# Layer 0's products in the edge stage of a four-layer graph network: first group of the fifth batch, or its third

## The chip, the cores and the metric

The kernel runs on one core of one Trainium2 chip, as one launch. The metric is the device time of the whole program in microseconds (us). TensorE is called PE here, VectorE DVE, ScalarE ACT, GpSimd POOL, SyncE SP, as the profile calls them.

## The reference, cut to what matters

Four graph layers over N = 3125 nodes with 128 features and E = 103125 directed edges (50000 drawn, both ways, and one loop for each node). Each layer is followed by a residual and a layer norm. Layer 0 is the one that matters here:

```python
xw = x @ weight
msgs = edge_val[:, None] * xw[edge_col]
out = jax.ops.segment_sum(msgs, edge_row, num_segments=N_NODES)
out = jax.nn.relu(out + b)
...
x = _layernorm(x + out)
```

Layer 1 is an attention layer over the same edges, layer 2 an attention layer that uses dot products, layer 3 two mean aggregations with products of weights.

## The kernel before

**Dense matrices in place of edges.** The kernel pads the nodes to 25 blocks of 128. It first turns the edge list into two 3200 x 3200 matrices in DRAM: `wd`, the edge weights in float32, one row for each target node, and `ctd`, the edge counts in bfloat16. After that every layer is a set of dense matrix products over these. For layer 0 the product is (block i of `wd`) transposed times (block i of `xw`), added up in PSUM over i = 0 to 24.

**The edge stage (lines 837 to 958).** The edges are sorted, and cut into 640 windows of five nodes (`WN = 5`). A batch is 16 windows, and the loop `for b in range(NBT)` (L897) has 40 batches; the last holds 4 windows. In each batch:

- `make(b + 1)` (called at the head of the loop) lets DVE build the one-hot matrices of the next batch: `ohd` and `ohc` (L865), then three `wod` (L876), which hold the weights in three bfloat16 parts. `ohd` and `ohc` have two buffers and `wod` has six, so DVE can be one batch ahead: the `ohd` of batch b + 2 needs that PE has read the `ohd` of batch b for the last time.
- The batch is worked through in four groups, k = 0, 4, 8 and 12, of four windows each. I write (b, k) for a group. PE makes the counts `cp` (8 matmuls, L911) and the weights `wp` (24 matmuls, L919). ACT copies them out as `cs` (L924) and `ws` (L930), and between the two it makes part of the next batch's `wod` (`cur[3](k)`, L882, four instructions). `cp` and `wp` share three PSUM buffers.
- After a batch, SP stores `ws` to `wd` (L941, two DMAs, 896 and 104 KB) and after each second batch `cs` to `ctd` (L944, 1000 KB).

**Layer 0's products inside the edge stage.** A row block of `wd` is complete as soon as the batches that hold its 128 rows are stored (80 rows a batch). So the stage already multiplies such blocks, on PE between the groups. `adds0` (L809 to 823) loads one row block into two tiles of ten column blocks (`cw`, L816, two DMAs of 640 KB, from a pool with four buffers) and returns 20 closures. Each is one product: a float32 matmul into PSUM at L820, which the trace shows as two passes. They go into the list `todo`. After each group the loop takes up to three from the head of the list and runs them. It then requests the next row block if the list holds 20 or fewer and the rows are stored:

```python
if order:
    m = min(3, len(todo)) if b > 3 else 0
    for f in todo[:m]:
        f()
    del todo[:m]

    if len(todo) <= 20 and (done + 1) * P <= (b - 1) * BW * WN:
        todo += adds0(zp, done, acc0, (0, Z0))
        done += 1
```

I call the two loads for one value of `done` "load 0" to "load 24". What the loop leaves over is run after it, and the remaining blocks follow (`for f in todo`, then `add0` for `range(done, NB)`). Then come layer 0's ends (`end0`), the products of the other five column blocks (`left`, also L820), and layer 1.

**What sets the order.** From the end of batch 2 on, PE and SP work in program order, written by hand (`manual_schedule`). The order on ACT and DVE is a planner's, which plans with its own cost model.

Of the kernel before, what the change touches and what calls it, by code (L numbers as in the profile page):

```python
# [510 lines left out]
def fast_path(  # L511
# [238 lines left out]
    def products_of_weights():  # L750
        nc.gpsimd.tensor_tensor(both, gb_row, sb_row, OP.add)
        tw = {}
        for name, w in (("l1", l1_wt), ("q", wqt), ("k", wkt), ("v", wvt)):
            t = zps.tile([P, P], F32, name="trw", tag="acc3")
            nc.tensor.transpose(t, w, ident)
            tw[name] = ep.tile([P, P], F32, name="tw_" + name)
            nc.scalar.copy(tw[name], t)
        t = zps.tile([P, P], F32, name="trw", tag="acc3")
        nc.tensor.matmul(t[:, 0 : 2 * H], tw["l1"], att, start=True, stop=True)
        nc.scalar.copy(watt, t[:, 0 : 2 * H])  # L760
        t = zps.tile([P, P], F32, name="trw", tag="acc3")
        nc.tensor.matmul(t, tw["q"], tw["k"], start=True, stop=True)
        nc.scalar.copy(wyv[:, 0:P], t)
        t = zps.tile([P, P], F32, name="trw", tag="acc3")
        nc.tensor.matmul(t, tw["v"], wot, start=True, stop=True)
        nc.scalar.copy(wyv[:, P:], t)

    def xw_of(b0, n):

        t = zps.tile([P, 512], F32, name="trx", tag="acc0")  # L770
        for k in range(n):
            nc.tensor.transpose(t[:, k * P : (k + 1) * P], x[:, b0 + k, :], ident)
        xT = ep.tile([P, 512], F32, name="f_xTb")
        nc.scalar.copy(xT[:, : n * P], t[:, : n * P])
        t = zps.tile([P, 512], F32, name="trx", tag="acc2")
        for k in range(n):
            nc.tensor.matmul(t[:, k * P : (k + 1) * P], xT[:, k * P : (k + 1) * P], l0_wt, start=True, stop=True)
        nc.scalar.copy(xw[:, b0 : b0 + n, :].rearrange("p b d -> p (b d)"), t[:, : n * P])
# [30 lines left out]
    def adds0(pool, i, accs, blocks):  # L809

        b0, n = blocks
        steps = []
        for h in range(0, n, 10):
            m = min(10, n - h)
            cw = pool.tile([P, min(10, n), P], F32, name="cw")[:, 0:m]
            nc.sync.dma_start(  # L816
                cw.rearrange("p c d -> p (c d)"), wd[i * P : (i + 1) * P, (b0 + h) * P : (b0 + h + m) * P]
            )
            for j in range(h, h + m):
                steps.append(lambda j=j, a=cw[:, j - h, :]: nc.tensor.matmul(  # L820
                    accs[j // 4][:, j % 4, :], a, xw[:, i, :], start=False,
                    stop=(i == NB - 1 and (j % 4 == 3 or j == n - 1)), skip_group_check=True,
                ))
        return steps
# [16 lines left out]
    def make(b):  # L841

        if b % 8 == 1 and 8 < b < NBT - 8:
            keys[b // 8 + 1] = columns_of(b // 8 + 1)
        if b % 8 == 3 and 8 < b < NBT - 8:
            keys[b // 8 + 1] = keys_of(*keys[b // 8 + 1])
        kd2, kc2, w2, w3 = keys[b // 8]
        ohd = op_.tile([P, 2 * BW, P], BF16, name="ohd")
        ohc = op_.tile([P, 2 * BW, P], BF16, name="ohc")

        def twos(k):
            k = k[:, b % 8, :, :, :].rearrange("p q w t -> p (q w) t")
            return k[:, :, None, :].to_broadcast([P, 2 * BW, P // 2, 2])

        def some(s):
            if b < NBT - 1:
                return [slice(0, 2 * BW if s < 2 else BW)]
            return [slice(0, LW)] + ([slice(BW, BW + LW)] if s < 2 else [])

        def packed(o, ww):  # L860
            return o[:, ww].rearrange("p w (a t) -> p w a t", t=2)

        for o, k in ((ohd, kd2), (ohc, kc2)):
            for ww in some(0):
                nc.vector.tensor_tensor(  # L865
                    packed(o, ww), twos(k)[:, ww],
                    ramp.rearrange("p (a t) -> p a t", t=2)[:, None, :, :].to_broadcast(
                        [P, ww.stop - ww.start, P // 2, 2]
                    ),
                    OP.is_equal,  # L870
                )
        wod = []
        for s in range(3):
            f = of_.tile([P, 2 * BW, P], BF16, name="wod")
            for ww in some(s):
                tip[s] = nc.vector.tensor_tensor(packed(f, ww), packed(ohd, ww), twos(w2[s])[:, ww], OP.mult)  # L876
            wod.append(f)

        def more(k):
            for w in range(k, k + 4):  # L880
                at = (b % 8) * BW + w
                nc.scalar.activation(wod[2][:, BW + w, :], ohd[:, BW + w, :], AF.Copy, scale=w3[:, 1, at : at + 1])  # L882

        return ohd, ohc, wod, more
# [4 lines left out]
    todo = []  # L889
# [6 lines left out]
    for b in range(NBT):  # L896
        ohd, ohc, wod, _ = cur  # L897
        cur = make(b + 1) if b + 1 < NBT else None
        nw = BW if b < NBT - 1 else LW
        if b % SB == 0:  # L900
            cs = sp.tile([P, NB, SB * BW * WN], BF16, name="cs")
            if b + SB == NBT:
                nc.gpsimd.memset(cs[:, :, ((SB - 1) * BW + LW) * WN :], 0.0)
        ws = sp.tile([P, BW, P], F32, name="ws")
        for k in range(0, nw, 4):
            cp = cps.tile([P, 4, P], F32, name="cp", tag="cw")
            wp = cps.tile([P, 4, P], F32, name="wp", tag="cw")
            for j in range(4):
                for q in range(2):
                    w = q * BW + k + j  # L910
                    nc.tensor.matmul(  # L911
                        cp[:, j, 0:KW], ohd[:, w, :], ohc[:, w, 0:KW], start=(j == 0 and q == 0), stop=(j == 3 and q == 1),
                        skip_group_check=True,
                    )
            for j in range(4):
                for q in range(2):
                    w = q * BW + k + j
                    for s in range(3):
                        made = nc.tensor.matmul(  # L919
                            wp[:, j, :], ohc[:, w, :], wod[s][:, w, :], start=(j == 0 and q == 0 and s == 0),  # L920
                            stop=(j == 3 and q == 1 and s == 2), skip_group_check=True,
                        )
            i0 = (b % SB) * BW * WN + k * WN
            nc.scalar.copy(  # L924
                cs[:, :, i0 : i0 + 4 * WN].rearrange("p c (w i) -> p c w i", i=WN),
                cp[:, :, 0:KW].rearrange("p w (i c) -> p c w i", c=NB),
            )
            if cur and (b + 1 < NBT - 1 or k < LW):
                cur[3](k)
            nc.scalar.copy(ws[:, k : k + 4, :], wp)  # L930
            if order:
                m = min(3, len(todo)) if b > 3 else 0
                for f in todo[:m]:
                    f()
                del todo[:m]
# [4 lines that stand above are left out]
        for a, e in ((0, 112), (112, KW)):  # L940
            nc.sync.dma_start(wv_[b * BW : b * BW + nw, a:e, :].rearrange("w k d -> k w d"), ws[a:e, 0:nw, :])  # L941
        if b % SB == SB - 1:
            i0 = (b - SB + 1) * BW * WN
            nc.sync.dma_start(ctd[:, :, i0 : i0 + SB * BW * WN].rearrange("c d i -> d c i"), cs)  # L944
        if b < 2:
            for blocks in GB[4 * b : 4 * b + 4]:
                xw_of(*blocks)
        if b == 2:
            with tc.issue_after(made.ins):
                products_of_weights()  # L950
            acc0 = [zps.tile([P, 4, P], F32, name=f"acc{k}", tag=f"acc{k}") for k in range(Z0 // 4)]
            for a in acc0:
                bias0(a, 4)

            order = ExitStack()
            order.enter_context(tc.manual_schedule(engines={mybir.EngineType.PE, mybir.EngineType.SP}))
# [446 lines left out]
    with ExitStack() as st:  # L1403
# [82 lines left out]
        for x_, (q, c) in enumerate(items):  # L1486
# [17 lines left out]
            elif c == NB - 1:  # L1504
                for k0 in range(0, n, 3):
                    m = min(3, n - k0)
# [3 lines left out]
                for k0 in range(0, n, 3):  # L1510
                    m = min(3, n - k0)
# [4 lines left out]
                    for j in range(m):  # L1516
                        b = i0 + k0 + j
# [258 lines left out]
```

## Time and profile before

| What | us |
|---|---|
| three runs, median (lowest to highest) | 1503.28 (1501.07 to 1508.55) |
| the profiled execution, its own time | 1507.44 |
| its span, first to last instruction | 1505.6 |
| PE busy / DVE busy / ACT busy in that span | 1395.4 / 978.8 / 914.3 |
| the first product of layer 0 on PE starts at | 88.07 |
| the edge stage's last group ends, with its products, at about | 463.9 |
| the last product into `acc0` ends at | 490.74 |

The profile gives each instruction's start and duration in us from the span's start. A row of the timeline merges equal neighbours (x24 is 24 instructions), and ends with the idle time of the engine before it and what ended that idle time, in brackets. The chain of waits is followed back from the last instruction: at each step it shows what the program was waiting for. The view by stretch gives, for each stretch of time, the busy time of the engines, the granted share of PE's clock (PEclk, 1.00 is full), the busy share of the DMA engines and the GB/s that they moved.

### The profile page before, as it was taken

Reading aid. Unit: us, or ns where it says so; the run is one execution under the profiler, and the core shown is the slowest. Engines: PE = TensorE matmul, PEld = TensorE weight load, DVE = VectorE, ACT = ScalarE, POOL = GpSimd, SP = SyncE. Lnnn points to the kernel's source line nnn. Section 1 sums busy time; section 2 is a strip of 40 time slices with the busy share of each in tenths; the row PEclk is TensorE's granted clock in tenths of the full one; section 3 lists DMA queues with packets and bytes.
Section 4 is the critical chain, followed back from the end, with each engine's and each line's share of the span. In section 5 each row is a group of like instructions: output and inputs, shape, how many; then the busy total and the mean of one; then the engine's idle time right before and its main releaser. Section 6 shows DMA issues by size and latency. Waiting matters only on the chain.

```text
span 1505.6 us, 34986 instructions
## 1 busy us (share of the span) xinstructions
PE 1395.4 (93%) x14775; PEld 1227.3 (82%) x14775; DVE 978.8 (65%) x1575; ACT 914.3 (61%) x1865; POOL 128.9 (9%) x164
## 2 busy tenths in 40 slices
PE   3889999999998988998979989899999999999996
PEld 3889999999998878987978989677777774458996
DVE  4989899999991389898888879534464352012005
ACT  2978789888882489878867787454555331023005
POOL 1000000000000012132032113200000000000000
PEclk8999999999999999999999999999999999999998
DMA  7368789989887733443433534332222218512551
GB/s 206 96 179 226 198 221 242 234 213 230 238 218 221 222 115 114 125 124 113 135 90 112 142 88 117 115 121 70 69 60 81 71 47 309 200 53 114 197 174 46
DMA packets 209700, 223.91 MB, mean 149 GB/s; under 512 B 72956, under 2 KB 183339, under 8 KB 209277
## 3 DMA queue, kind: packets, MB, share of 16 engines
q1 hardware_dynamic: 208748, 218.51, 50.6%
q8 instruction: 117, 1.92, 0.5%
q0 software_dynamic: 400, 1.97, 0.4%
q10 hardware_dynamic: 385, 1.11, 0.2%
q14 instruction: 50, 0.41, 0.1%
HBM read 157.19 MB, written 64.36 MB: 147 GB/s over the span
## 4 chain that ended last, share of the span: by engine, by line
PE 72%; DVE 11%; ACT 8%; DMA 4%; issue 2%; POOL 2%; SPq 0%; ACTq 0%; DVEq 0%; POOLq 0%
PE wp L919 10%; PE acc L1302 9%; PE acc L1453 9%; PE s L1445 8%; PE acc L1553 7%; PE acc L1629 6%; PE acc L820 6%; PE acc L1297 5%; PE cp L911 3%; DVE cm L1287 3%; ACT wod L882 3%; PE left L820 2%; DMA cw<-wd 2%; ACT fm L1286 1%; DVE cm L1280 1%
## 5 line engine op out<-in xcount | busy, mean ns | idle before, releaser
L1302 PE MATMUL acc<-vp,cm 128*128 128x198 bf16 x2500 | 344.5, 252 | 8.2 <-DVE cm L1287 6.7
L1297 PE MATMUL acc<-vp,ct 128*128 128x204 bf16 x1250 | 317.1, 255 | 10.1 <-DVE vp L1205 4.5
L1286 ACT ACTIVATE fm<-adr,bas 128x768 bf16<-128x768 f32 (+1 forms) x320 | 287.2, 953 | 61.9 <-DVE cm L1287 60.1
L1302 PEld LDWEIGHTS <-cm 128*128 128x128 bf16 x2500 | 236.4, 98 | 25.2 <-DVE cm L1287 8.8
L919 PE MATMUL wp<-wod,ohc 128*128 128x128 bf16 x3768 | 239.6, 220 | 7.1 <-ACT cs L924 5.4
L919 PEld LDWEIGHTS <-ohc 128*128 128x128 bf16 x3768 | 220.9, 99 | 8.7 <-issue 8.3
L876 DVE TENSOR_TENSOR wod<-ohd,w 128x4096 bf16<-128x4096 bf16 (+2 forms) x122 | 221.4, 1867 | 0.4 <-PE wp L919 0.4
L1287 DVE TENSOR_TENSOR cm<-fm,ct 128x768 bf16<-128x768 bf16 (+1 forms) x320 | 202.6, 664 | 28.8 <-PE acc L1302 13.9
L882 ACT ACTIVATE wod<-ohd,wu 128x128 bf16<-128x128 bf16 x628 | 197.7, 397 | 0.0
L1449 DVE TENSOR_TENSOR e<-e,ct 128x416 f32<-128x416 f32 (+1 forms) x175 | 108.0, 623 | 110.4 <-ACT e L1448 102.8
L1448 ACT ACTIVATE e<-s,f_nm 128x416 f32<-128x416 f32 (+1 forms) x175 | 109.6, 633 | 103.1 <-PE s L1445 95.7
L1453 PEld LDWEIGHTS acc<-self__8043,e 128*128 128x128 f32 x1250 | 148.2, 192 | 19.8 <-issue 18.9
L820 PE MATMUL acc<-f_xw,cw 128*128 128x128 f32 x1000 | 147.8, 289 | 11.9 <-DMA cw<-wd 11.9
L1453 PE MATMUL acc<-self__8043,e 128*128 128x129 f32 x1250 | 148.5, 276 | 0.0
L1445 PE MATMUL s<-yT,f_xT 128*128 128x416 f32 (+1 forms) x350 | 143.1, 544 | 4.5 <-ACT rt L1425 2.6
L820 PEld LDWEIGHTS acc<-f_xw,cw 128*128 128x128 f32 x1000 | 127.7, 198 | 12.5 <-DMA cw<-wd 12.5
L1297 PEld LDWEIGHTS <-ct 128*128 128x128 bf16 x1250 | 122.1, 98 | 4.0 <-issue 2.7
L924 ACT CAST cs<-cp 128x500 bf16<-128x500 f32 x157 | 90.7, 578 | 39.5 <-PE cp L911 39.5
L1445 PEld LDWEIGHTS s<-yT,f_xT 128*128 128x128 f32 x350 | 62.5, 191 | 55.4 <-issue 40.7
L865 DVE TENSOR_TENSOR ohd<-kd,ramp 128x4096 bf16<-128x4096 bf16 (+1 forms) x41 | 90.1, 2200 | 20.3 <-PE cp L911 18.6
L930 ACT COPY ws<-wp 128x512 f32<-128x512 f32 x157 | 90.2, 579 | 20.9 <-PE wp L919 20.6
L911 PE MATMUL cp<-ohc,ohd 128*128 128x125 bf16 x1256 | 96.3, 220 | 3.7 <-ACT ws L930 3.5
(341 smaller groups left out, 1520.6 us busy)
## 6 DMA issues: line engine op xcount, KB each, us to landing
ct<-f_ctd SPq DMA_DIRECT2D x46, 800.0 KB
wd<-ws SPq DMA_DIRECT2D x39, 896.0 KB
cw<-wd SPq DMA_DIRECT2D x50, 640.0 KB
ct<-f_ctd SPq DMA_DIRECT2D x150, 192.0 KB
f_ctd<-cs SPq DMA_DIRECT2D x20, 1000.0 KB
ct<-f_ctd SPq DMA_DIRECT2D x50, 224.0 KB
ct<-f_ctd SPq DMA_DIRECT2D x25, 416.0 KB
ct<-f_ctd SPq DMA_DIRECT2D x25, 365.2 KB
```

The costliest lines, as they stand in the source:

```text
L820: steps.append(lambda j=j, a=cw[:, j - h, :]: nc.tensor.matmul(accs[j // 4][:, j % 4, :], a, xw[:, i, :], start=False, stop=(i == NB - 1 a ...
L876: tip[s] = nc.vector.tensor_tensor(packed(f, ww), packed(ohd, ww), twos(w2[s])[:, ww], OP.mult)
L882: nc.scalar.activation(wod[2][:, BW + w, :], ohd[:, BW + w, :], AF.Copy, scale=w3[:, 1, at : at + 1])
L911: nc.tensor.matmul(cp[:, j, 0:KW], ohd[:, w, :], ohc[:, w, 0:KW], start=(j == 0 and q == 0), stop=(j == 3 and q == 1), skip_group_check=True,)
L919: made = nc.tensor.matmul(wp[:, j, :], ohc[:, w, :], wod[s][:, w, :], start=(j == 0 and q == 0 and s == 0), stop=(j == 3 and q == 1 and s ...
L1286: nc.scalar.activation(f[:, : n * P], at, AF.Relu, bias=bas[:, c, h : h + 1], scale=UP)
L1287: nc.vector.tensor_tensor(m[:, : n * P], f[:, : n * P], ct[:, : n * P], OP.min)
L1297: nc.tensor.matmul(out_(F1, PW), ct[:, k * P : (k + 1) * P], vp[:, c, hp : hp + 2, :, 2 * F1 : V1], start=(c == 0), stop=False, skip_group ...
L1302: nc.tensor.matmul(out_(0, 2 * F1)[:, j], ms[j][:, k * P : (k + 1) * P], vp[:, c, hp + j, :, 0 : 2 * F1], start=False, stop=(c == NB - 1 a ...
L1445: nc.tensor.matmul(s[:, :m], xT[:, c * P : (c + 1) * P], yT[:, i0 * P + a : i0 * P + a + m], start=True, stop=True)
L1448: nc.scalar.activation(e[:, a : a + m], s[:, :m], AF.Exp, bias=nm[:, q : q + 1], scale=scale)
L1453: nc.tensor.matmul(acc[k // 3][:, (k % 3) * (P + 1) : (k % 3 + 1) * (P + 1)], es[q, c][:, k * P : (k + 1) * P], vo[:, c, 0 : P + 1], start ...
```

## The change

The products begin at group (4, 8) in place of (4, 0). The pair (b, k) is compared as Python compares tuples, so groups (4, 8), (4, 12) and all groups of later batches are in, and (4, 0) and (4, 4) are not.

```diff
             if order:
-                m = min(3, len(todo)) if b > 3 else 0
+                m = min(3, len(todo)) if (b, k) > (4, 4) else 0
                 for f in todo[:m]:
                     f()
                 del todo[:m]
```

Nothing is added to or taken from the computation: the same 500 products run in the same order, six of them later.

## The prediction

> **What bounds the kernel now.** I read the chain of waits first: PE holds 72% of it, and in the edge stage two of its longest pieces are not work but transfers of `cw`:
>
> ```profile
> 100.02 7.29 DMA cw<-wd
> ...
> 136.90 10.70 DMA cw<-wd
> ```
>
> Then PE's timeline around these two:
>
> ```profile
> 101.31 0.60 PE L911 MATMUL cp<-ohc,ohd 128*128 128x125 bf16 x8
> ...
> 103.09 0.66 PE L820 MATMUL acc<-f_xw,cw 128*128 128x128 f32 x4
> 107.35 0.80 PE L820 MATMUL acc<-f_xw,cw 128*128 128x128 f32 x2 [3.59 <-DMA cw<-wd]
> ...
> 112.64 0.60 PE L911 MATMUL cp<-ohc,ohd 128*128 128x125 bf16 x8
> ...
> 142.68 0.60 PE L911 MATMUL cp<-ohc,ohd 128*128 128x125 bf16 x8
> ...
> 147.64 1.65 PE L820 MATMUL acc<-f_xw,cw 128*128 128x128 f32 x6 [3.02 <-DMA cw<-wd]
> ...
> 153.70 0.60 PE L911 MATMUL cp<-ohc,ohd 128*128 128x125 bf16 x8
> ```
>
> The reader is to see that the third product of group (5, 8) waits for load 1, and the first of (9, 0) for load 3. Between them PE has no wait over 0.15 us. Then the view by stretch, for the clock after a wait and for the steady state:
>
> ```profile
> 107.40:112.60 5.20, 5.20 (x40) 5.14 (x41) 3.31 (x2) 1.16 (x2) 0.00 (x0) 0.51 0.01 5
> ...
> 166.00:169.00 3.00, 1.98 (x29) 1.80 (x27) 2.76 (x6) 3.00 (x10) 0.00 (x0) 1.00 0.93 183
> ...
> 180.00:200.00 20.00, 20.00 (x307) 19.91 (x305) 20.00 (x11) 17.34 (x49) 0.00 (x0) 1.00 0.89 228
> ```
>
> The seventh number is the granted clock: about half for the 5 us behind the first wait, and full across an idle time of 1.02 us (166 to 169). The last row is the steady state: PE and DVE are both busy for all 20 us. A group starts each 2.505 us on PE, so a batch takes 10.02; DVE makes a batch in 10.0 (2.20 + 2.20 + 5.6). So what PE gains counts only as far as DVE follows, and I need DVE's idle times, from its timeline:
>
> ```profile
> 109.09 2.29 DVE L865 TENSOR_TENSOR ohd<-kd,ramp 128x4096 bf16<-128x4096 bf16 x1 [3.89 <-PE cp L911]
> ...
> 111.58 2.29 DVE L865 TENSOR_TENSOR ohc<-kc,ramp 128x4096 bf16<-128x4096 bf16 x1 [0.20 <-PE wp L919]
> ...
> 120.86 2.29 DVE L865 TENSOR_TENSOR ohd<-kd,ramp 128x4096 bf16<-128x4096 bf16 x1 [1.45 <-ACT wod L882]
> ...
> 156.91 2.29 DVE L865 TENSOR_TENSOR ohd<-kd,ramp 128x4096 bf16<-128x4096 bf16 x1 [5.99 <-PE cp L911]
> ```
>
> These are all of DVE's waits between 85.3 and 168; from there to 250 it waits 0.24 in all.
>
> **The change, part by part.** *What moves.* No instruction or DMA is added or removed. Six products (12 passes) leave groups (4, 0) and (4, 4), and the list is six longer from then on. I followed `todo` by hand through both versions. Load 1 is requested at (5, 0) in both, but needed at (6, 0) instead of (5, 8); load 3 is requested at (8, 0) in both, and needed at (9, 8) instead of (9, 0). So each gets two groups more, 5.0 us. From load 2 on, each load has 6 or 7 groups between request and need (before: 4 to 7). Many later requests come one to three groups later, because the list must first fall to 20. At the end 417 products are taken instead of 423, and the list holds 23 after (39, 0): load 22, requested at (38, 12) before, now comes after the loop, in SP's queue behind the stores of batches 38 and 39 and the last `ctd` store.
>
> *What the waits cost PE.* From the `cp` of (5, 8) to that of (6, 0) 112.64 - 101.31 = 11.33 us pass where 2 x 2.505 = 5.01 are normal: 6.32, of which 3.59 is the wait and the rest the half clock. From (9, 0) to (9, 8) it is 153.70 - 142.68 - 5.01 = 6.01. Sum 12.3, and the six products give another 2 x 0.72 = 1.45 at the front, where 0.72 is the chain's piece for six passes.
>
> [...]
>
> *Whether the waits go.* DVE starts batch 5 at 85.22, before the first product at 88.07, so this start stays. With no waits it goes on without a break: batch 6 is made at 105.2, as now. PE then runs `wp` of (6, 0) to 106.6, and its third product comes at about 107.0. Load 1 landed at 100.02 + 7.29 = 107.31. Its issue follows batch 4's store, which waits for ACT's last `ws` of batch 4; this can be 0 to 1.45 earlier. So load 1 lands at 105.9 to 107.3, and a wait of 0 to 0.3 is left: short enough to keep the clock, by the 1.02 above. Load 3: batch 9 is made at 105.2 + 30.1 = 135.3, so the first product of (9, 8) comes at 135.3 + 5.0 + 1.3 = 141.6. Its issue came 2.2 after the last `ws` of batch 7 started; that `ws` now starts at about 124.2, so the issue is at 126.4, and with the same 10.7 it lands at 137.1, with 4.5 to spare.
>
> *What DVE leaves of it.* DVE can win back its idle times, 3.89 + 0.20 + 1.45 + 5.99 = 11.5, and no more, since it runs on without a break to 250. PE could give 13.8, so DVE is the bound: batch 11's `ohd` starts at 145.4 instead of 156.9, and the stage runs 11.5 earlier from there. Later waits (PE for ACT's `cs` or `ws`, 0.5 to 1.0 each) stay. The end of the loop comes 11.5 earlier; if later stretches in which PE leads let it use its 2.3 of advance, up to 12.
>
> *The tail of layer 0.* The rows of PE's timeline:
>
> ```profile
> 463.22 4.68 PE L820 MATMUL acc<-f_xw,cw 128*128 128x128 f32 x40
> 467.74 1.28 PE L807 MATMUL left<-l_br,ones 128*128 128x128 f32 x10
> 468.85 4.63 PE L820 MATMUL acc<-f_xw,cw 128*128 128x128 f32 x40
> 478.79 11.95 PE L820 MATMUL acc<-f_xw,cw 128*128 128x128 f32 x80 [5.30 <-DMA cw<-wd]
> ```
>
> Today 40 products run, then PE waits 5.30 for load 23, and 40 more follow in 11.95 (the first at half clock). After the change, and in the clock of before, 26 run, PE is ready at 470.2, waits for load 22, and then has 60: 11.95 + 20 x 0.226 (4.52 us for 40 passes at full clock in the chain) = 16.5. When does load 22 land? At the latest when load 23 did, at 478.8: the end is then 495.3, which is 4.5 later than 490.74. But load 23 had load 22's 1.28 MB ahead of it in the queue, and load 22 does not: at the 413 GB/s of the stretch 478 to 481 that is 3.1, so it lands at about 475.5 and the end is 492.0, 1.3 later. At best the stores also start a little earlier (the issue of load 22 held SP from 456.59 to 462.0) and the cost is 0. The value is 1.0, ends 0 and 4.5. Load 24 needs load 22's buffers, free about 4.5 to 8 us after PE resumes, and is needed 12 us after: with 4 us from issue to landing in an empty queue it is in time.
>
> [...]
>
> *Sum.* -11.5 + 1.0 = -10.5, from 1507.44 to 1496.9 for a profiled execution. The median of the runs is 4.16 below the profiled time; the same step gives 1503.28 - 10.5 = 1492.8. Behind layer 0 everything shifts; where half-clock windows fall may change, so I allow 2 us either way.
>
> **The rivals.** *Part stays.* Load 1 still lands over 1 us late and the clock halves again (the spare is only 0), or the tail pays 4.5. The first costs at most 6.3, less the 2.3 that PE has in hand, so 4; either way the gain is about 7, together 3: 1496 to 1500. For it speaks the thin spare of load 1; against it, that its issue can only move forward.
>
> *The waits only move.* Requests hang on the same list, so loads come as much later as their products, and DMA is busy 0.89 of the time: 1503. Against it: loads 1 and 3 are held by the rows stored, not by the list.
>
> *Slower: ACT's order.* The planner orders ACT anew; where it puts four or eight `wod` in front of a `cs` or `ws` that PE needs, PE waits about 1.0 (as before the `cp` at 168.23), and the profile has ten such waits of 0.4 to 1.0 in the stage. If from (5, 0) on one came in each batch, 34 would cost up to 34 us, 24 more than now; it decides from about 11 more on. With 16 more: -10.5 + 16, 1509. Against it: with loads earlier, ACT's steady pattern (eight, four, four) should hold longer.
>
> **How the numbers follow.** Forecast 0.60, part stays 0.20, the waits only move 0.08, slower 0.12. The forecast's own range is 1490 to 1496. Faster or slower by over 0.5% (7.5 us) is about what a measurement of this kernel can tell from no change. The forecast gives 0.58 of faster and part stays 0.08, so 0.66; ACT's order gives 0.10 of slower; the rest, 0.24, is within. For 8 in 10 the range holds the forecast with 2 us below and part stays: 1487 to 1501.
>
> **What would show it.** Right: no wait for `cw` at L820 over 0.5 us between 100 and 160; the granted clock full there; DVE's 3.89 and 5.99 gone; batch 11's `ohd` at about 145.4; 26 products, one wait of 3 to 6 us and 60 products in the tail. Wrong: a wait over 1 us at (6, 0); DVE waits for PE as before; more ACT waits of 1 us than ten; a tail over 2 us longer.

## The result, and the profile after

| | before | after |
|---|---|---|
| median of 22 runs each (lowest to highest), us | 1505.61 (1501.07 to 1508.83) | 1510.00 (1504.96 to 1512.22) |
| the profiled execution: own time / span | 1507.44 / 1505.6 | 1509.99 / 1508.2 |
| start of batch 4 on PE | 86.29 | 86.88 |
| start of batch 39, counted from that of batch 4 | 375.15 | 374.15 |
| from there to the end of the last product into `acc0` | 29.30 | 30.49 |
| from there to the end of the span | 1014.90 | 1016.67 |

The ratio after to before is 1.0029, 95% interval 1.0021 to 1.0036: a little slower, where 10.5 us less was forecast. The rows from batch 4 on split the difference of the two spans: +0.6 before the products begin, -1.0 in the loop, +1.2 in the tail, +1.8 behind it. The loop, the tail and the part behind it are taken up below; no run explains the +0.6.

**The waits for `cw` are gone.** PE's timeline of the kernel after, around the first products of loads 1 and 3, which belong to (6, 0) and (9, 8). Load 1's is the third of the products that start at 107.83:

```profile
106.05 0.60 PE L911 MATMUL cp<-ohc,ohd 128*128 128x125 bf16 x8
...
107.83 0.89 PE L820 MATMUL acc<-f_xw,cw 128*128 128x128 f32 x6
...
141.10 0.60 PE L911 MATMUL cp<-ohc,ohd 128*128 128x125 bf16 x8
141.54 1.50 PE L919 MATMUL wp<-wod,ohc 128*128 128x128 bf16 x24
142.88 0.89 PE L820 MATMUL acc<-f_xw,cw 128*128 128x128 f32 x6
```

Batch 6 starts at 106.05 instead of 112.64, and no row has a bracket with a wait. DVE's timeline of the kernel after:

```profile
105.71 2.28 DVE L865 TENSOR_TENSOR ohd<-kd,ramp 128x4096 bf16<-128x4096 bf16 x1
...
145.48 2.28 DVE L865 TENSOR_TENSOR ohd<-kd,ramp 128x4096 bf16<-128x4096 bf16 x1
```

These two `ohd` started at 109.09 and 156.91 before, behind idle times of 3.89 and 5.99; now they come without one. The chain of waits says the same: between 85 and 148 it now goes through DVE alone.

```profile
85.81 2.29 DVE ohd L865
...
95.84 2.20 DVE ohd L865
...
145.56 2.20 DVE ohd L865
```

**Where the gain went.** Counted from batch 4, batches 11 to 16 start 12.0 earlier than before. Then it is given back in steps: 10.1 is left at batch 17, 6.4 at batch 19, 5.6 at batch 23, 1.2 at batch 27, 0.1 at batch 31 and 1.0 at batch 39. PE's waits from 85 to 500 us (engine, line, what it waited for: us in total, times, longest), the kernel before first, then the kernel after:

```profile
PE acc L820 <- DMA cw<-wd: 11.9, 3, 5.3
PE wp L919 <- ACT cs L924: 3.3, 4, 1.0
PE cp L911 <- ACT ws L930: 3.2, 4, 1.0
PE wp L919 <- ACT ws L930: 1.6, 2, 1.0
```

```profile
PE wp L919 <- ACT ws L930: 6.9, 5, 3.1
PE acc L820 <- DMA cw<-wd: 5.4, 1, 5.4
PE wp L919 <- ACT cs L924: 4.8, 6, 1.0
PE cp L911 <- ACT ws L930: 3.7, 4, 1.9
```

The waits for `cw` fall from 11.9 to 5.4; the waits for ACT grow from 8.1 (ten) to 15.4 (fifteen). The largest two stand in batches 18 and 26, in which the columns of keys are made for the next eight batches. PE's timeline and ACT's, both of the kernel after, in batch 18:

```profile
237.66 0.60 PE L911 MATMUL cp<-ohc,ohd 128*128 128x125 bf16 x8
240.95 2.04 PE L919 MATMUL wp<-wod,ohc 128*128 128x128 bf16 x24 [2.69 <-ACT ws L930]
```

```profile
235.75 0.58 ACT L924 CAST cs<-cp 128x500 bf16<-128x500 f32 x1
237.07 0.40 ACT L706 CAST w<-wt 128x256 bf16<-128x256 f32 x1 [0.74 <-DVE wt L705]
237.38 0.40 ACT L706 CAST w<-wu 128x256 bf16<-128x256 f32 x1
237.68 2.15 ACT L882 ACTIVATE wod<-ohd,wu 128x128 bf16<-128x128 bf16 x7
239.74 0.39 ACT L706 CAST w<-wu 128x256 bf16<-128x256 f32 x1
240.03 0.40 ACT L882 ACTIVATE wod<-ohd,wu 128x128 bf16<-128x128 bf16 x1
240.34 1.04 ACT L930 COPY ws<-wp 128x512 f32<-128x512 f32 x2
```

Two `ws` stand behind three casts, the first of which waits 0.74 for DVE, and eight `wod`. `cp` and `wp` share three PSUM buffers, so PE waits 2.69 us for one. In the kernel before, ACT's order in this batch has one `ws` ahead of the eight `wod` (which start at 247.51) and one behind them (at 249.86). ACT's row of the first `ws`, then PE's rows with its only wait in that batch, 0.55:

```profile
245.10 0.60 ACT L930 COPY ws<-wp 128x512 f32<-128x512 f32 x1
```

```profile
247.25 0.60 PE L911 MATMUL cp<-ohc,ohd 128*128 128x125 bf16 x8
...
250.47 0.60 PE L911 MATMUL cp<-ohc,ohd 128*128 128x125 bf16 x8 [0.55 <-ACT ws L930]
```

No line of the diff touches ACT. But the planner plans ACT and DVE anew for every program, and its order on ACT differs from batch 4 on. Batches 16, 24 and 34 now have `cs cs`, eight `wod`, `cs`, eight `wod`, `ws ws ws`; before, only batch 32 had that.

The clock adds to it. By stretch (us; PE, PEld, DVE, ACT and POOL busy; PEclk; DMA share; GB/s), the kernel after:

```profile
107.40:112.60 5.20, 5.20 (x83) 5.18 (x81) 5.20 (x4) 4.67 (x14) 0.00 (x0) 1.00 0.77 199
...
241.70:245.20 3.50, 3.50 (x31) 3.44 (x29) 0.00 (x0) 2.50 (x8) 0.00 (x0) 0.51 0.26 48
```

The half clock that stood behind the wait for `cw` (0.51 from 107.4 on, before) is gone, and one stands behind the wait for `ws` in its place (0.50 from 241.73 to 245.15); another follows the 3.07 us wait of batch 26 (0.50 from 330.48 to 333.89). From the start of batch 11 to that of batch 39, PE's idle time grows from 7.1 to 13.7, and the busy time of the same 4268 matmul records from 283.6 to 288.0. These 6.6 and 4.4 make up the 11.0 that the loop gave back. Of the 4.4, the two half-clock stretches of 3.4 can take up to 1.7 each (an estimate: half of each); no row places the other 1.0.

**The tail.** PE's timeline of the kernel after:

```profile
462.81 6.02 PE L820 MATMUL acc<-f_xw,cw 128*128 128x128 f32 x52
468.67 1.28 PE L807 MATMUL left<-l_br,ones 128*128 128x128 f32 x10
475.32 16.20 PE L820 MATMUL acc<-f_xw,cw 128*128 128x128 f32 x120 [5.37 <-DMA cw<-wd]
```

As forecast: 26 products (52 passes), a wait for load 22, and 60 products.

### The profile page after: what moved, and what is told of

It is laid out like the page before. It is cut to its first block, busy times and chain, and to the rows that moved or that the text cites. A ratio compares the mean times of both kernels' runs of the same rounds, so it can differ in the third digit from the quotient of the medians.

```text
span 1508.2 us, 34965 instructions
## 1 busy us (share of the span) xinstructions
PE 1395.4 (93%) x14762; PEld 1225.0 (81%) x14775; DVE 976.2 (65%) x1575; ACT 913.0 (61%) x1865; POOL 129.8 (9%) x164
## 4 chain that ended last, share of the span: by engine, by line
PE 69%; DVE 14%; ACT 9%; issue 3%; DMA 2%; POOL 2%; SPq 0%; ACTq 0%; DVEq 0%; POOLq 0%
PE acc L1453 9%; PE wp L919 9%; PE acc L1302 9%; PE s L1445 8%; PE acc L1553 7%; PE acc L1629 6%; PE acc L820 6%; PE acc L1297 4%; ACT wod L882 4%; DVE cm L1287 3%; PE cp L911 3%; DVE wod L876 2%; PE left L820 2%; ACT fm L1286 1%; DVE ohd L865 1%
## 5 line engine op out<-in xcount | busy, mean ns | idle before, releaser
L1297 PEld LDWEIGHTS <-ct 128*128 128x128 bf16 x1250 | 122.1, 98 | 4.0 <-issue 2.7
L1629 PEld LDWEIGHTS <-ct 128*128 128x128 bf16 x1725 | 96.9, 98 | 0.0
```

Source lines behind the costliest of these rows:

```text
L1297: nc.tensor.matmul(out_(F1, PW), ct[:, k * P : (k + 1) * P], vp[:, c, hp : hp + 2, :, 2 * F1 : V1], start=(c == 0), stop=False, skip_group ...
L1629: nc.tensor.matmul(acc[g][:, j, :], ct[:, (b0 + j) * P : (b0 + j + 1) * P], ups[b // 4][:, b % 4, s, :], start=(b == 0 and s == 0 and j == ...
```

## The experiments

Two theories were set against each other. ORDER: the change itself is worth what was forecast, and the new order on ACT gives it back. PACE: the work takes this time in any order; what PE gains in one place it waits for in another. Times of batches are counted from the start of batch 4 and given against the kernel before.

**The order held fixed.** ACT and DVE also work in program order, and that order is written by hand: in each batch `cs ws cs`, eight `wod`, `ws cs`, four, `ws cs`, four, `ws`, which is the commonest order of the kernel before. The making of the key columns is cut into steps, which stand between these (not shown; in the diff, the engines' names are shortened and the comments are added). e1 has the start of before, e2 that of after, all else alike:

```diff
-    order.enter_context(tc.manual_schedule(engines={PE, SP}))
+    order.enter_context(tc.manual_schedule(engines={PE, SP, Activation, DVE}))
...
         def more(k):
-            for w in range(k, k + 4):
+            if k in later_:        # steps of the key columns, in batches 10, 18, 26
+                later_[k]()
+            if k == 0 and whole:   # whole: a batch of 16 windows behind the third
+                return
+            for w in range(0 if k == 4 and whole else k, k + 4):
```

e1, hand order, start at (4, 0). Expected:

> The kernel before, with ACT and DVE also in an order written by hand from batch 3 on: in each batch cs, ws, cs, eight wod, ws, cs, four wod, ws, cs, four wod, ws, which is the planner's own commonest order. Theory ORDER (the changed kernel lost its gain because the planner put ws and cs behind eight or more wod in more batches): the two waits for cw stay (3.6 and 3.0 us, half clock behind each), but PE's later waits for ACT go from ten (7.9 us) to about three, in the batches with keys (11, 19, 27). So 1500 to 1505 us, 1 to 5 below the kernel before. Rival PACE (DVE and ACT cannot follow a PE that has no early waits, whatever their order; the early waits cost nothing): as many ACT waits as before, 1505 with 2 either way.

e2, hand order, start at (4, 8). Expected:

> The changed kernel with the same order by hand on ACT and DVE. ORDER: no wait for cw before the tail, and what is gained by batch 11 (about 11 us against e1) is still there at group (39, 0); the tail costs 1.2. So 8 to 12 us below e1, 1489 to 1496. PACE: the gain of batch 11 is given back by batch 39 as in the changed kernel, through PE waits for ACT or DVE: within 3 us of e1.

Measured: e1 1497.78 (1495.14 to 1503.64), ratio to before 0.9957 (0.9942 to 0.9971); e2 1496.07 (1491.80 to 1498.28), 0.9943 (0.9925 to 0.9962). Both forecasts missed: e1 fell 2.2 below its range, and e2, named 8 to 12 below e1, is 1.7 below it, just outside its own range. By the medians alone that is PACE, "within 3 us of e1". The split shows otherwise: batch 39 starts 8.7 earlier in e1 and 16.7 earlier in e2, and behind batch 11 e2's gain never falls more than 0.4 below the 11.4 that it has there. So with a fixed order the change keeps 8.0 in the loop. The tail takes 3.6 of it (27.87 in e1, 31.47 in e2), the time behind the tail is 2.6 longer, and batch 4 starts 0.5 later. ORDER is right for the loop; both further terms needed an answer.

**The second group.** The planner's own order, start at (4, 4):

```diff
-                m = min(3, len(todo)) if (b, k) > (4, 4) else 0
+                m = min(3, len(todo)) if (b, k) >= (4, 4) else 0
```

> The products begin at the second group (4, 4); ACT and DVE ordered by the planner, as in before and after. The waits for cw should shrink to about 1.1 and 0.5 us by the same working (3.6 and 3.0 less one group of 2.5), with no half clock, so 8 to 10 us are gained by batch 11. The planner's order here has three ws behind sixteen wod in batches 24 and 32, and two or three ws behind eight to twelve in 16, 26, 34 and 36; the kernel before has such batches in 24, 32, 34 and 36 only. ORDER: two more such batches at 1.5 to 4 us each, so 3 to 8 us are given back: 1498 to 1504. PACE: all is given back: 1505 to 1510.

Measured: 1503.81 (1502.74 to 1508.95), ratio 0.9999 (0.9985 to 1.0013). The median lies in ORDER's range, but the runs show no difference from the kernel before. In the profile, batch 11 starts 10.8 earlier, batch 39 still 5.7; before batch 4 and in the tail 0.9 each is lost. This order has only one wait of 3 us (3.17, batch 26), and the gain falls by 2.1 there. In the loop one wait for `cw` is left, 1.33 long, with full clock behind it.

**The tail.** e2 with four products in place of three in six groups near the end, so that load 22 is requested inside the loop again:

```diff
-                m = min(3, len(todo)) if (b, k) > (4, 4) else 0
+                m = min(4 if (36, 0) <= (b, k) <= (37, 4) else 3, len(todo)) if (b, k) > (4, 4) else 0
```

> As e2, and groups (36, 0) to (37, 4) take four products instead of three, so that the list is as in the kernel before from (37, 4) on and load 22 is again requested at (38, 12). If the tail of layer 0 costs the changed kernel 1.2 us (29.3 us from the cp of (39, 0) to the last product before, 30.5 after), this is 0.5 to 1.5 below e2. If PE has no room for six more products there, it is the same as e2.

Measured: 1494.45 (1491.47 to 1495.49), ratio 0.9930 (0.9914 to 0.9947), 1.6 below e2. The tail is 27.58, 3.9 shorter than in e2 and like e1's: the longer tail came from the six products left over. The six groups cost 1.3 in the loop, and up to batch 12 e4 lost 1.6 against e2: a half-clock stretch stands at 157.8 in e4, and none in e2, behind waits of 2.25 and 2.24 (more on this below).

**The fifth batch.** The planner's order, start at (5, 0):

```diff
-                m = min(3, len(todo)) if (b, k) > (4, 4) else 0
+                m = min(3, len(todo)) if (b, k) >= (5, 0) else 0
```

> Before, with the start at (5, 0) instead of (4, 0), and the planner's own order on ACT and DVE. ORDER (the gain is given back where the planner's order makes PE wait for ACT): the two waits for cw are gone as after the change, batch 11 starts 11 to 12.5 earlier, and the gain falls where ACT's order has eight wod in front of ws: in batches 17, 19, 27, 29, 31 and 37 (counted by the one whose wod are made), by 1 to 3 each; (39, 0) starts 2 to 7 earlier, the median is 1501 to 1508. PACE (PE takes the same time whatever the order, it only moves): the gain falls slowly and in every batch alike. Twelve products fewer than before are taken in the stage, so the tail is 1 to 3 longer. [...]

Measured: 1511.31 (1505.61 to 1512.88), ratio 1.0033 (1.0018 to 1.0047). The median lies 3 above the forecast range. Batch 11 starts 11.2 earlier; at batch 17 9.0 are left, at 19 5.4, at 27 3.1, at 39 2.1. The steps came where ACT's order had said: 1.9 at batch 17, 4.0 at 19, 1.6 at 27, 1.1 at 29 and at 31, 0.8 at 37. That at 19 is larger than the 1 to 3 expected, with half clock behind a wait of 3.06. The tail is 32.23, 2.9 longer than before, the end of the 1 to 3 that was named. The profiled span is 4.4 longer: 1.1 ahead of batch 4, 2.1 less in the loop, 2.9 more in the tail and 2.4 more behind it.

**ACT alone by hand.** e2 with DVE's order left to the planner:

```diff
-    order.enter_context(tc.manual_schedule(engines={PE, SP, Activation, DVE}))
+    order.enter_context(tc.manual_schedule(engines={PE, SP, Activation}))
```

> e2 (start at (4, 8), hand order) with the hand order on ACT alone; DVE's order is left to the planner. If ACT's order is what gave the gain back: as e2, batch 11 to 39 within 2 of e2's starts, median 1494 to 1498. If DVE's order (the key columns' wt and wu between the wod) is the cause: PE waits of 2 to 3 us at batches 11, 19 and 27 come back, median 1500 to 1508.

Measured: 1491.27 (1487.70 to 1492.78), ratio 0.9905 (0.9883 to 0.9928). Batches 11 to 31 start 12.0 to 13.2 earlier and batch 39 18.2, 1.5 more than in e2. The median lies 2.7 below the range named for ACT's order. So it is ACT's order: with that alone in hand (and the key columns cut into steps, as in e1 and e2), and DVE left to the planner, no more than 0.3 is given back at any step behind batch 11. Its waits from 85 to 500:

```profile
PE acc L832 <- DMA cw<-wd: 5.9, 1, 5.9
PE cp L953 <- ACT ws L972: 4.3, 3, 2.2
```

Three waits for ACT, where the kernel after has fifteen (L953 is its `cp`, L972 its `ws`).

**The key columns' batches, and the change alone in the best order.** e6 is e4 with four `wod` behind the second `cs`, four behind the third and eight behind the fourth in batches 10, 18 and 26. e8 has the same order with the start at (4, 0) and no groups of four products:

```diff
-            for w in range(0 if k == 4 and whole else k, k + 4):
+            lo = 0 if k == 4 and whole else k
+            if steps:              # batches 10, 18, 26
+                lo = k - 4 if k < 12 else 8
+            for w in range(lo, k if steps and k < 12 else k + 4):
```

> e4 (hand order on ACT and DVE, start at (4, 8), four products a group from (36, 0) to (37, 4)) with another order in the three batches that also make the columns of keys: four wod after the second cs, four after the third and eight after the fourth, in place of eight, four and four. ORDER: PE's wait for the second ws in these batches falls from 1.47 to 0 to 0.5, and from 2.24 to about 1.1 in the first; DVE's 0.71 behind each goes; (39, 0) starts 1.5 to 4 earlier than in e4, and the median is 1490.5 to 1493.5. PACE: within 1 of e4, 1493.5 to 1495.5. [...]

> The order of e6 with the start at (4, 0) as in before and without the four-product groups: the change taken alone, in the best order found. ORDER: the waits for cw are back (about 2.2 and 2.9 as in e1), the loop is 7 to 9 longer than in e6 up to batch 28, and the tail is about as long as in e6; median 4 to 8 above e6, 1496 to 1500. If the change is worth nothing at a fixed order: within 2 of e6.

Measured: e6 1489.26 (1488.11 to 1491.20), ratio 0.9895 (0.9874 to 0.9916), the fastest of all; e8 1494.95 (1493.93 to 1496.46), 0.9933 (0.9911 to 0.9954). Both fell below their ranges. The wait for the second `ws` fell from 1.45 to 0.3, and in the first such batch from 2.25 to 1.07. Batch 39 starts 4.0 earlier than in e4. Against e8, e6 has 4.7 less in the loop, 0.4 less in the tail, 0.5 less behind it, and 5.7 less in the median: at a fixed order the change, with the six groups that mend its tail, pays. Up to batch 36 the loop is 6.1 shorter, less than the 7 to 9 that were named for batch 28; the six groups take 1.3 of it. It pays less than 11.5. One reason is in the rows: with ACT's order steady the two waits for `cw` are shorter already, 2.20 and 2.80 in e8 in place of 3.59 and 3.02, and only the first has half clock behind it.

**Half clock behind the waits.** In e8 two waits for `cw` differ in this. PE's timeline, then by stretch:

```profile
106.27 0.79 PE L832 MATMUL acc<-f_xw,cw 128*128 128x128 f32 x2 [2.20 <-DMA cw<-wd]
...
145.39 0.94 PE L832 MATMUL acc<-f_xw,cw 128*128 128x128 f32 x6 [2.80 <-DMA cw<-wd]
```

```profile
102.64:106.05 3.41, 1.43 (x21) 1.24 (x18) 2.88 (x2) 2.64 (x8) 0.00 (x0) 1.00 0.92 328
106.05:109.46 3.41, 3.19 (x27) 3.13 (x28) 1.45 (x1) 1.52 (x5) 0.00 (x0) 0.50 0.11 45
...
140.18:143.60 3.42, 2.41 (x38) 2.23 (x36) 3.42 (x2) 2.28 (x6) 0.00 (x0) 1.00 0.87 189
143.60:147.01 3.41, 1.62 (x22) 1.61 (x23) 3.41 (x3) 0.21 (x1) 0.00 (x0) 1.00 1.00 351
147.01:150.42 3.41, 3.41 (x58) 3.40 (x56) 2.40 (x2) 3.41 (x11) 0.00 (x0) 1.00 1.13 353
```

The shorter wait, 2.20, has half clock behind it (0.50 from 106.05), the longer one, 2.80, has not (1.00 from 147.01). The bounds of the rows lie whole numbers of 3.413 us from 106.05, where the half clock starts. Between them the first wait leaves PE 1.98 us idle in one step (3.41 less 1.43); the second is cut at 143.60 into 1.01 and 1.79. The same step is found in the profiles of before and after: between 60 and 1200 us each has nine half-clock stretches, and all start a whole number of 3.413 us after the first one (105.72 in before, 241.73 in after), to 0.03 of that unit. Cut into these steps, from 90 to 1180 us, the two profiles have 23 steps at full clock with 1.00 to 1.76 us idle that were followed by full clock. Of the 18 that were followed by half, 16 had 1.96 to 3.41 idle. The other two, with 0.82 (before, from 491.42) and 1.18 (after, from 490.91), stand around the end of the last product into `acc0` or just behind it, where PE does transposes and matmuls only 8 wide.

The first half-clock stretch, less whole units, stands 3.32 us from the start in before, 2.80 in after and 0.24 in e8. These are kernels with one profiled execution each, so no run shows how far this moves between two executions of one kernel. The time behind the last product into `acc0`, in the ten profiles (before, after, e1 to e8):

| time to the end, us | kernels |
|---|---|
| 1016.67 to 1018.32 | after, e2, e4, e5 |
| 1013.05 | e7 |
| 1014.46 to 1015.04 | before, e1, e3, e6, e8 |

In all ten the instructions there stand in the same order on each engine (PE's by its weight loads, since 13 matmul records are missing in five traces). The last product ends 12.97 us behind the start of a half-clock stretch in before (490.74 and 477.77) and 17.68 behind one in after (491.52 and 473.84), 3.80 and 5.18 of the unit. Whether that place sets the time behind it was not shown: no run moved it alone.

## Why the prediction was wrong, by its own steps

- **Whether the waits go: right.** No wait for `cw` between 100 and 160, the clock full there (1.00), `ohd` at 145.48 where 145.4 was forecast.
- **What DVE leaves of it: right.** Batch 11 started 12.0 earlier counted from batch 4, and 11.4 in the profile's own time; the forecast was 11.5, up to 12.
- **"Later waits (PE for ACT's `cs` or `ws`, 0.5 to 1.0 each) stay": this step failed.** It carried the order of the trace before over to a program for which the planner makes a new one. The waits went from ten with 8.1 in all to fifteen with 15.4, two of them 2.69 and 3.07, and 11.0 of the 12.0 were gone at batch 39. So the term of -11.5 was -1.0 at the loop's end. With ACT's order fixed the gain stays (e2, e7).
- **The rival "Slower: ACT's order" was the right mechanism with too small a chance.** It "decides from about 11 more on", that is 11 more waits of 1.0. Only five more came, but they are longer and two have half clock behind them, and the loop gave back 11.0 us. Its picture was off: not one wait of 1.0 in each batch, but few long ones, most of it (7.8 us) in the batches that make key columns, 18 and 26. The argument against it, that earlier loads would hold ACT's steady pattern longer, had no row behind it: the planner goes by its own cost model, not by the trace.
- **The tail: right, but for another loop than the one forecast.** 1.19 against 1.0, PE resumed at 475.32 against 475.5. But the step was made "in the clock of before" for a loop that should end 11.5 earlier, and (39, 0) came only 0.4 earlier, so the close fit is partly luck. Where the loop kept its gain (e2 against e1), the tail took back 3.6. Counted from (39, 0), the load that PE waits for landed 3.1 earlier in after than before (14.3 against 17.4), but only 1.3 earlier in e2 than in e1 (14.9 against 16.2), while the 20 more products behind it cost 4.3 and 4.9. By that pair the forecast for a kept loop would have been about 8 and not 10.5, an estimate (11.5 less 3.6).
- **Behind layer 0: inside its bound.** +1.8 where 2 either way was allowed. The order of instructions there is unchanged, and kernels with the start at (4, 8) lie on both sides of before (1013.05 in e7, 1014.46 in e6, 1016.67 in after), so it is likely not the change's own.
- **The clock: right in what it took from the trace, but the length of a wait does not tell.** "Short enough to keep the clock, by the 1.02 above" agrees with the runs where it was used: in after no wait is left at (6, 0), and the clock is 1.00 from 100 to 160. In e8 a wait of 2.20 has half clock behind it (0.50) and one of 2.80 full clock (1.00), so the bound that the prediction drew from a wait's length does not carry to waits of this size.

What stays open: the medians of before and after differ by 4.4 and the two profiled executions by 2.55. The execution profiled before lies 1.8 above its kernel's median; no run shows why. That a planner's order equal to before's, with the start at (4, 8), keeps the 12 us was not tried as such; e2 and e7 hold another fixed order.

## What to carry to other kernels

Where some engines work in a planner's order, an edit on another engine can change that order, so list the new order of every planned engine before carrying a trace's waits over: a wait found in the old trace is no constant. Hold the order fixed to measure a small move. And follow a gain to the stage that comes next: a loop that ends earlier meets the same transfers at its tail, so a part of the gain can be lost there (PE waits 4.16 for the load in e1 and 5.98 in e2).

## What the runs showed of the hardware

In the profiles of before and after, between 60 and 1200 us, PE's half-clock stretches start whole numbers of 3.413 us apart, from 105.72 on in before and from 241.73 on in after. From 90 to 1180 us, 16 of the 18 steps of that length that were followed by half clock had 1.96 to 3.41 us of idle time, the other two 0.82 and 1.18; the 23 steps at full clock with 1.00 to 1.76 idle were followed by full clock. In e8 a wait of 2.20 us has half clock behind it (0.50) and one of 2.80 full clock (1.00). With the same work in the same order behind layer 0, the ten profiles differ by up to 5.3 us there (1013.05 to 1018.32), half of what this change was forecast to gain.
